# Waiting gathers and pairwise sums ahead of the transposes in a four-layer graph attention kernel

## Chip, cores and metric

The kernel runs on one core of a Trainium2 chip. The metric is the device time of one execution in microseconds (us), lower is better. Before the change it is 2476.21 us, the median of 11 runs (2470.24 to 2486.74).

## What is computed

A graph of 3327 nodes has features `x` (3327 x 256, float32) and a sparse adjacency matrix `adj` (3327 x 3327, int32, about 0.5% ones). Four layers run one after the other. Layer 0 is a graph attention with one score per neighbour. Layers 1 to 3 are transformer layers whose attention is masked by the graph. Cut to what matters:

```python
# layer 0
h = x @ Wt.T + bt
s = leaky_relu(h @ Wa.T + ba, 0.2)
w = softmax(where(adj > 0, s, -9e15), axis=1)
x = layernorm(x + (w @ h) @ Wp.T + bp)
# layers 1, 2, 3 (8 heads of 32)
q, k, v = split(layer_norm(x) @ w_qkv)
scores = where(adj != 0, q @ k.T * 32 ** -0.5, -inf)   # per head
out = softmax(scores) @ v                               # per head
x = x + out @ w_proj + b_proj
x = x + gelu(layer_norm(x) @ w1 + b1) @ w2 + b2
```

Row i of `out` is a sum over the neighbours of node i alone: each neighbour's 256 values, weighted per head.

## The kernel before

**Layer 0 and the lists.** The first part reads `adj` whole, computes layer 0, and makes for every node a list of its neighbours. The nodes are sorted by the number of neighbours and cut into 26 blocks of 128; `CAPS` has the longest list of each block, from 34 down to 9, 430 in all. Keys and values of layer 1 are written to a table in DRAM with one row of 512 floats (2 KB) per node, keys first.

**Attention by gathers.** Layers 1 to 3 work through the blocks in the order `ORDER`: lists of middle length first, rising to the longest, and the two blocks with the shortest lists last. For slot k of a block's lists, one indirect DMA that GpSimd issues (L640) fetches for each of the 128 nodes the table row of its k-th neighbour: 128 rows of 2 KB, a tile column of 128 x 512. A block's slots are cut into groups of 3 or 4 (`cuts`), 118 groups in a layer and 354 in all, and each group has a tile out of a pool of 12 (`SLOTS`). `Attend` has the steps of one block:

- `gather(g)` issues the group's 3 or 4 gathers.
- `scores(g)`: VectorE multiplies the keys by the query in place (L651) and sums over each head (L652).
- `exps` and `shares`: the softmax over the block's slots (L655 to L672). `shares` also opens the accumulator `po` in PSUM with a matrix product of zeros (L674).
- `values(oT, j)`: VectorE multiplies the group's values by their weights in place (L684). Then TensorE transposes each slot's two halves of 128 x 128 into the same `po`, adding up (L687). So the sum over neighbours is made by TensorE: two transposes a slot, 860 in a layer and 2580 in all. After the last group ScalarE copies `po` out (L693).

**The tail.** Blocks go on in pairs, the last two alone. `tail` is a generator that adds the projection, the norm, the feed-forward products (L567, L580) and, for layers 1 and 2, the keys and values of the next layer, which a scatter puts into the next table (L602). In layer 3 a scatter writes the output instead (L589). The norms raise to the power of -0.5 on GpSimd (L120). Pieces of tails are interleaved by `turn`.

**The order.** It is written out by hand in `layer` (`tc.manual_schedule`). Turn `now` handles one group: first the gathers of all groups up to `now + 3` (`AHEAD`) for which a slot tile is free are issued, then come `scores` of group `now`, a piece of each waiting tail, and `values` of the block before, spread over the turns. Each engine runs its instructions in this order. GpSimd's stream holds the gathers, in layer 1 the loads of node rows (L496), the powers, and the scatters. Each of its indirect DMAs signals its landing on one of eight semaphores in turn, and a gather waits for the one that used its semaphore before it, eight DMAs back.

Of the kernel before, what the change touches and what calls it, by code (L numbers as in the profile page):

```python
# [20 lines left out]
D = 256  # L21
# [25 lines left out]
SG = 4  # L47
SLOTS = 12
AHEAD = 3
NODES = 5  # L50
FH = FF // P // 2

# [5 lines left out]
def kernel(ctx: ExitStack, tc: tile.TileContext, ins, out: bass.AP):  # L58
    nc = tc.nc

    def wt(L, name):
        return ins[f"L{L}_gnn_{name}"]
# [47 lines left out]
    def moments(views, name):  # L110

        n = len(views)
        mv = small.tile([P, 4, 2], FP, tag="mv", name=f"mv_{name}")
        for j, v in enumerate(views):
            st = small.tile([P, 6], FP, tag="st", name=f"st_{name}_{j}")
            nc.vector.bn_stats(st, v)  # L116
            nc.vector.bn_aggr(mv[:, j, :], st)
        r = small.tile([P, 4], FP, tag="rsig", name=f"rsig_{name}")
        nc.vector.tensor_scalar(r[:, :n], mv[:, :n, 1], EPS, None, ALU.add)
        nc.gpsimd.tensor_tensor(r[:, :n], r[:, :n], mhalf[:, :n], ALU.pow)  # L120
        return mv, r

    def normed(pool, views, mv, rs, name):

        n = len(views)
        nm = small.tile([P, 4], FP, tag="nmu", name=f"nmu_{name}")
        nc.vector.scalar_tensor_tensor(nm[:, :n], mv[:, :n, 0], -1.0, rs[:, :n], ALU.mult, ALU.mult)  # L127
        xns = []
        for j, v in enumerate(views):
            xn = pool.tile([P, D], FP, tag="xn", name=f"xn_{name}_{j}")  # L130
            nc.scalar.activation(xn, v, AF.Identity, bias=nm[:, j:j + 1], scale=rs[:, j:j + 1])  # L131
            xns.append(xn)
        return xns
# [38 lines left out]
    with ExitStack() as st:  # L172
# [11 lines left out]
        for L in LAYERS:  # L184
            o = 16 * (L - 1)
            for k, name in ((0, "g1"), (2, "be1"), (4, "g2"), (6, "be2"), (8, "b1")):
                n = wt(L, name).shape[0] // P
# [71 lines left out]
        for g, blocks in enumerate(GROUPS):  # L259
            n = len(blocks)  # L260
# [210 lines left out]
    with ExitStack() as st:  # L471
# [12 lines left out]
        idx = keep.tile([P, NB, LW], U32, name="idx")  # L484
# [8 lines left out]
        def node_rows(b):  # L493

            nodes_[b] = work.tile([P, NODE], FP, tag="node", bufs=NODES, name=f"node_{b}")
            nc.gpsimd.indirect_dma_start(  # L496
                out=nodes_[b], out_offset=None, in_=node_dr[:, :],
                in_offset=bass.IndirectOffsetOnAxis(ap=perm[:, b:b + 1], axis=0))

        def node_list(b):  # L500

            t = nodes_[b]
            cd = t[:, 2 * D:2 * D + CAND]
            nr = (CAPS[b] + 7) // 8
            w = 8 * nr

            cg = work.tile([P, CAND], FP, tag="cg", name=f"cg_{b}")
            nc.vector.scalar_tensor_tensor(cg, cd, 0.0, segb.rearrange("p s k -> p (s k)"), ALU.is_gt, ALU.mult)
            nc.vector.tensor_add(cg, cg, cd)
            ls = work.tile([P, LW], FP, tag="ls", name=f"ls_{b}")  # L510
            for k in range(nr):
                nc.vector.max(out=ls[:, 8 * k:8 * k + 8], in_=cg)
                if k < nr - 1:
                    nc.vector.match_replace(out=cg, in_to_replace=ls[:, 8 * k:8 * k + 8], in_values=cg, imm_value=0.0)
            em = work.tile([P, LW], FP, tag="em", name=f"em_{b}")
            own = work.tile([P, 1], FP, tag="own", name=f"own_{b}")
            nc.vector.tensor_scalar(em[:, :w], ls[:, :w], 0.5, None, ALU.is_lt)
            nc.vector.tensor_scalar(own, pf[:, b:b + 1], 1.0, None, ALU.add)
            nc.vector.scalar_tensor_tensor(ls[:, :w], em[:, :w], own, ls[:, :w], ALU.mult, ALU.add)
            nc.vector.tensor_scalar(idx[:, b, :w], ls[:, :w], -1.0, None, ALU.add)  # L520
            nc.vector.tensor_scalar(bias[:, b, :w], em[:, :w], NEG, None, ALU.mult)
            nc.vector.tensor_reduce(found[:, b, 0:1], em[:, :w], AX.X, ALU.add)
            nc.scalar.copy(found[:, b, 1:2], t[:, 2 * D + CAND:])
            nc.scalar.copy(x_sb[:, b, :], t[:, :D])
# [8 lines left out]
        def tail(L, w, wqn, blocks, oT):  # L533
# [15 lines left out]
            mv, rs = moments(views, f"f{tag}")  # L549
            yield AHEAD  # L550
            xns = normed(work, views, mv, rs, f"f{tag}")
# [41 lines left out]
            mv, rs = moments(views, f"h{tag}")  # L593
            yield AHEAD
            xns = normed(work, views, mv, rs, f"h{tag}")
# [20 lines left out]
        class Attend:  # L616
# [19 lines left out]
            def gather(self, g):  # L636
                a, z = self.cuts[g]
                t = slots.tile([P, SG, 2 * D], FP, tag="slot", name=f"sl_{self.tag}_{g}")
                for k in range(a, z):
                    nc.gpsimd.indirect_dma_start(  # L640
                        out=t[:, k - a, :], out_offset=None, in_=kv_dr[self.L][:, :],
                        in_offset=bass.IndirectOffsetOnAxis(ap=idx[:, self.b, k:k + 1], axis=0))
                self.tiles.append(t)

            def scores(self, g):
# [31 lines left out]
            def values(self, oT, j):  # L677

                g = self.vdone
                a, z = self.cuts[g]  # L680
                n = z - a
                t = self.tiles[g]
                vv = t[:, :n, D:].rearrange("p s (h d) -> p s h d", h=HEADS)
                nc.vector.tensor_mul(vv, vv, self.pw[:, a:z, :, None].to_broadcast([P, n, HEADS, HD]))  # L684
                for k in range(n):
                    for c in range(2):
                        nc.tensor.matmul(self.po[:, c, :], t[:, k, D + c * P:D + (c + 1) * P], ident,  # L687
                                         is_transpose=True, start=False,
                                         stop=(a + k == self.S - 1 and c == 1))
                self.vdone += 1  # L690
                if self.vdone < len(self.cuts):
                    return False
                nc.scalar.copy(oT[:, :, j * P:(j + 1) * P], self.po)  # L693
                return True

        place = {b: (m, j) for m, blocks in enumerate(CHUNKS) for j, b in enumerate(blocks)}
        tails = []
        hidden = []

# [9 lines left out]
        def layer(L):  # L709
# [10 lines left out]
            if first:  # L720
                for b in ORDER[:NODES - 2]:
                    node_rows(b)
# [17 lines left out]
            for k, a in enumerate(att):  # L740
# [3 lines left out]
                for g in range(n):  # L744
                    if first and g == 0:
                        if k + NODES - 2 < NB:
                            node_rows(ORDER[k + NODES - 2])
                        for m in ((1, 2) if k == 0 else (k + 2,)):
                            if m < NB:
                                node_list(ORDER[m])  # L750
                    while sent < turns and held < SLOTS and sent - now <= AHEAD:
                        todo[sent][0].gather(todo[sent][1])
# [219 lines left out]
```

## Time and profile before

| | |
|---|---|
| median of 11 runs | 2476.21 us |
| the profiled execution | 2476.94 us |
| its span, first to last instruction | 2475.1 us |
| VectorE (DVE) busy | 1781.7 us, 72% |
| TensorE (PE) matrix products busy | 1663.3 us, 67% |
| GpSimd (POOL) busy | 1442.7 us, 58% |
| ScalarE (ACT) busy | 769.1 us, 31% |
| gathers (L640) | 1290, 3.7 us median from issue to landing |
| software DMA queue | 363.51 MB, 50.0% of the 16 engines' span |

The profile shows one execution, with times in us from the start of the span. Busy time is the time in which an engine ran an instruction of the program; a DMA that GpSimd issues is busy on GpSimd while it makes the DMA's descriptors, and the transfer itself runs on the 16 DMA engines. `out<-in` names the tile written and the tiles read; `sl` is a group's tile, `kv` a table of keys and values, `po` the sum over neighbours. A bracket at the end of a timeline row has the idle time of the engine ahead of the instruction, and what ended it; "issue" there means that the engine waited for nothing that the profile shows. A time from issue to landing runs from the start of the instruction on GpSimd to the semaphore that tells that all the data are there.

### The profile page before, as it was taken

What the parts mean: (1) busy time and instruction counts of PE and PEld (TensorE: products, weight loads), DVE (VectorE), ACT (ScalarE), POOL (GpSimd) and SP (SyncE); (2) the same over time, 40 slices, a digit from 0 to 9 for tenths busy, and PEclk for the clock granted to TensorE, in tenths of its full rate; (3) what the DMA queues carried; (4) which work ended last, traced back from release to release, by engine and by line L of the source; (5) the groups of instructions that cost most, each with busy time, mean ns of one, the idle gap of its engine ahead of it and who ended that gap; (6) DMA issues with size and microseconds to landing.
All of it is one profiled execution on the core that took longest, in us unless ns stands there. A gap on an engine that the chain in (4) does not pass through costs nothing. (4 is left out here: it accounts for less than half of the span.)

```text
span 2475.1 us, 25607 instructions
## 1 busy us (share of the span) xinstructions
PE 1663.3 (67%) x8349; PEld 1303.3 (53%) x8349; DVE 1781.7 (72%) x3203; ACT 769.1 (31%) x1420; POOL 1442.7 (58%) x1632
## 2 busy tenths in 40 slices
PE   5687851666786667682787787767826767766566
PEld 5556530555565555561565565555625655544455
DVE  3898956877778888726867878787357777777772
ACT  2787820223332222240332422232302322211222
POOL 0111116766667777517766777776167777777761
PEclk9899975687888887795788888778957878877778
DMA  6466416756567777507766677776076666666660
GB/s 236 152 231 214 149 66 194 209 169 191 178 193 206 209 212 209 157 32 255 202 194 195 187 218 214 209 212 183 26 221 201 202 192 200 199 202 184 198 182 11
DMA packets 154568, 451.22 MB, mean 182 GB/s; under 512 B 30576, under 2 KB 57850, under 8 KB 151098
## 3 DMA queue, kind: packets, MB, share of 16 engines
q0 software_dynamic: 111168, 363.51, 50.0%
q1 hardware_dynamic: 38462, 80.03, 9.4%
q10 hardware_dynamic: 4794, 5.94, 0.7%
q8 instruction: 69, 1.13, 0.2%
q14 instruction: 75, 0.61, 0.1%
HBM read 410.48 MB, written 38.88 MB: 182 GB/s over the span
## 5 line engine op out<-in xcount | busy, mean ns | idle before, releaser
L640 POOL DMA_INDIRECT sl<-kv,idx x1290 | 1230.7, 954 | 405.6 <-issue 322.9
L687 PE MATMUL po<-ident,sl 128*128 128x128 f32 x2580 | 475.7, 348 | 603.2 <-DVE sl L684 602.5
L687 PEld LDWEIGHTS po<-ident,sl 128*128 128x128 f32 x2580 | 397.6, 181 | 672.4 <-DVE sl L684 623.3
L651 DVE TENSOR_TENSOR sl<-sl,qp 128x1024 f32<-128x1024 f32 (+1 forms) x354 | 397.0, 1121 | 229.5 <-DMA sl<-kv,idx 172.0
L652 DVE TENSOR_REDUCE sc<-sl 128x32 f32<-128x1024 f32 (+1 forms) x354 | 398.2, 1125 | 12.0
L684 DVE TENSOR_TENSOR sl<-sl,qp 128x1024 f32<-128x1024 f32 (+1 forms) x354 | 389.0, 1119 | 2.6
L567 PE MATMUL pu<-fT,w 128*128 128x256 f32 (+1 forms) x1344 | 326.0, 391 | 38.0 <-ACT fT L143 38.0
L580 PE MATMUL pd<-w,gT 128*128 128x256 f32 x1248 | 324.0, 416 | 24.4 <-ACT gT L571 24.4
L580 PEld LDWEIGHTS pd<-w,gT 128*128 128x128 f32 x1248 | 256.2, 211 | 75.4 <-ACT gT L571 28.3
L567 PEld LDWEIGHTS pu<-fT,w 128*128 128x128 f32 x1344 | 253.9, 205 | 78.3 <-ACT fT L143 46.8
L571 ACT ACTIVATE gT<-pu,pv 128x256 f32<-128x256 f32 (+1 forms) x336 | 135.0, 456 | 267.3 <-PE pu L567 266.5
L161 PE MATMUL pk<-wq,hT 128*128 128x512 f32 x312 | 167.7, 664 | 3.1 <-ACT hT L143 3.1
L131 ACT ACTIVATE xn_f<-x_sb,nmu_f,rsig_f 128x256 f32<-128x256 f32 x78 | 42.8, 593 | 361.3 <-DVE nmu_f L127 347.3
L585 DVE TENSOR_TENSOR x_sb<-x_sb,pd 128x512 f32<-128x512 f32 (+1 forms) x42 | 27.2, 648 | 164.4 <-PE pd L580 164.4
L693 ACT COPY oT<-po 128x256 f32<-128x256 f32 x78 | 29.0, 372 | 373.4 <-PE po L687 373.1
L548 DVE TENSOR_TENSOR x_sb<-x_sb,pp 128x512 f32<-128x512 f32 (+1 forms) x42 | 27.2, 648 | 129.1 <-PE pp L546 129.0
L423 DVE MAX8 cand<-abf 128x8 f32<-128x256 bf16 x338 | 119.1, 410 | 0.0
L401 POOL MEMSET abf<- 128x1 bf16 x26 | 2.5, 100 | 192.9 <-DVE cand L423 165.2
L602 POOL DMA_INDIRECT kv<-kvr,perm x52 | 52.3, 1005 | 90.2 <-ACT kvr L163 78.3
L413 ACT ACTIVATE aT<-pt 128x1024 bf16<-128x1024 bf16 x104 | 85.0, 874 | 13.9 <-PE pt L412 13.9
L161 PEld LDWEIGHTS pk<-wq,hT 128*128 128x128 f32 x312 | 61.9, 215 | 51.5 <-issue 36.9
L166 PE MATMUL pq<-wq,hT 128*128 128x256 f32 x312 | 83.6, 392 | 7.2 <-ACT kvr L163 7.2
(217 smaller groups left out, 1959.4 us busy)
## 6 DMA issues: line engine op xcount, KB each, us to landing
a<-in_adj_dram SPq DMA_DIRECT2D x25, 1663.5 KB
sl<-kv,idx POOLq DMA_INDIRECT x1290, 3.7
kv<-kvr SPq DMA_DIRECT2D x26, 256.0 KB
q<-qr SPq DMA_DIRECT2D x52, 128.0 KB
q<-q SPq DMA_DIRECT2D x52, 128.0 KB
w<-in_L_gnn_w_dram SPq DMA_DIRECT2D x6, 1024.0 KB
node<-x SPq DMA_DIRECT2D x26, 128.0 KB
node<-qr SPq DMA_DIRECT2D x26, 128.0 KB
```

The costliest lines, as they stand in the source:

```text
L161: nc.tensor.matmul(pk, hT[:, c, :], wq[:, c, D:], start=(c == 0), stop=(c == 1))
L166: nc.tensor.matmul(pq[:, :D], hT[:, c, :], wq[:, c, :D], start=(c == 0), stop=(c == 1))
L413: nc.scalar.activation(aT[:, k0:k0 + kn, :], pt[:, :kn, :], AF.Sign)
L423: nc.vector.max(out=cand[:, 8 * m:8 * m + 8], in_=ab3[:, m, :])
L567: nc.tensor.matmul(pu[:, a, :n * P], w["w1"][:, c, f * P:(f + 1) * P], fT[:, c, :n * P], start=(c == 0), stop=(c == 1))
L571: nc.scalar.activation(gT[:, f0 + a, :n * P], pu[:, a, :n * P], AF.Gelu_apprx_tanh, bias=pv[:, L - 1, 8 + f:9 + f])
L580: nc.tensor.matmul(pd[:, j, :], gT[:, f, j * P:(j + 1) * P], w["w2"][:, h * FH + f, :], start=False, stop=(h == 1 and f == FH - 1 and j == ...
L640: nc.gpsimd.indirect_dma_start(out=t[:, k - a, :], out_offset=None, in_=kv_dr[self.L][:, :], in_offset=bass.IndirectOffsetOnAxis(ap=idx[:, ...
L651: nc.vector.tensor_mul(kq, kq, self.qp[:, None, :D].to_broadcast([P, n, D]))
L652: nc.vector.tensor_reduce(self.sc[:, a:z, :], kq.rearrange("p s (h d) -> p s h d", h=HEADS), AX.X, ALU.add)
L684: nc.vector.tensor_mul(vv, vv, self.pw[:, a:z, :, None].to_broadcast([P, n, HEADS, HD]))
L687: nc.tensor.matmul(self.po[:, c, :], t[:, k, D + c * P:D + (c + 1) * P], ident, is_transpose=True, start=False, stop=(a + k == self.S - 1 ...
```

## The change

It has two parts. First, a list `flight` holds the gathers issued last. From the third gather on, each one waits for the landing of the gather two before it. The list runs on over groups, blocks and layers; node loads and scatters are not in it. Second, after the values of a group are weighted, VectorE adds the last n // 2 slots of the group's n to its first n // 2 in place. For a group of four, two slots are left; for a group of three, the third is added to the first, and two are left. Only these are transposed into `po`.

```diff
+FLIGHT = 2
...
                 for k in range(a, z):
-                    nc.gpsimd.indirect_dma_start(
+                    ins = nc.gpsimd.indirect_dma_start(
                         out=t[:, k - a, :], out_offset=None, in_=kv_dr[self.L][:, :],
-                        in_offset=bass.IndirectOffsetOnAxis(ap=idx[:, self.b, k:k + 1], axis=0))
+                        in_offset=bass.IndirectOffsetOnAxis(ap=idx[:, self.b, k:k + 1], axis=0)).ins
+                    if len(flight) == FLIGHT:
+                        tc.add_manual_dep(ins, flight.pop(0).name,
+                                          mybir.DependencyInfo(mybir.DependencyClass.Sync, mybir.DependencyReason.DATA),
+                                          reason="gathers in flight")
+                    flight.append(ins)
                 self.tiles.append(t)
...
                 nc.vector.tensor_mul(vv, vv, self.pw[:, a:z, :, None].to_broadcast([P, n, HEADS, HD]))
-                for k in range(n):
+                m = n // 2
+                nc.vector.tensor_add(t[:, :m, D:], t[:, :m, D:], t[:, n - m:n, D:])
+                for k in range(n - m):
                     for c in range(2):
                         nc.tensor.matmul(self.po[:, c, :], t[:, k, D + c * P:D + (c + 1) * P], ident,
                                          is_transpose=True, start=False,
-                                         stop=(a + k == self.S - 1 and c == 1))
+                                         stop=(z == self.S and k == n - m - 1 and c == 1))
...
+        flight = []
         tails = []
```

## The prediction

> **What bounds the kernel now.** I read the groups of instructions first, then the gather line by itself, then GpSimd's timeline, and last the busy time by layer. The groups (busy us, mean ns of one, idle time before and its releaser):
>
> ```profile
> L640 POOL DMA_INDIRECT sl<-kv,idx x1290 | 1230.7, 954 | 405.6 <-issue 322.9
> L687 PE MATMUL po<-ident,sl 128*128 128x128 f32 x2580 | 475.7, 348 | 603.2 <-DVE sl L684 602.5
> L684 DVE TENSOR_TENSOR sl<-sl,qp 128x1024 f32<-128x1024 f32 (+1 forms) x354 | 389.0, 1119 | 2.6
> ```
>
> The gathers hold GpSimd for 1230.7 us, and most of its idle time ahead of them, 322.9 us, has no cause that the profile shows. The timeline of GpSimd in layer 1 tells what that is:
>
> ```profile
> 1003.48 0.95 POOL L640 DMA_INDIRECT sl<-kv,idx  x1 [0.30 <-issue]
> 1004.73 0.95 POOL L640 DMA_INDIRECT sl<-kv,idx  x1 [0.30 <-issue]
> 1005.98 0.94 POOL L640 DMA_INDIRECT sl<-kv,idx  x1 [0.30 <-issue]
> ```
>
> A gather is 0.95 us of work and 0.30 us of gap, so one starts every 1.25 us, with no wait for any landing. A gather is in the air for longer than that; the gather line by itself says how long:
>
> ```profile
> L640 POOL DMA_INDIRECT sl<-kv,idx x1290: 942/949/1194, 391.7 to 2407.6; - x185
> DMA to landing us min/median/max: 3.3/3.7/6.5
> ```
>
> 3.7 us counts from the start of the issue. VectorE's first product of layer 1 confirms it: it starts 3.78 us after the start of its group's last gather.
>
> ```profile
> 394.19 1.01 POOL L640 DMA_INDIRECT sl<-kv,idx  x1 [0.30 <-issue]
> ...
> 397.97 0.95 DVE L651 TENSOR_TENSOR sl<-sl,qp 128x768 f32<-128x768 f32 x1 [1.74 <-DMA sl<-kv,idx]
> ```
>
> So about three gathers fly at once (3.7 / 1.25). The streams, first gather to last, are seen in these rows (and 391.7 and 2407.6 above):
>
> ```profile
> 1040.53 0.95 POOL L640 DMA_INDIRECT sl<-kv,idx  x1 [0.30 <-issue]
> ...
> 1119.92 0.99 POOL L640 DMA_INDIRECT sl<-kv,idx  x1 [2.94 <-issue]
> ...
> 1727.95 0.95 POOL L640 DMA_INDIRECT sl<-kv,idx  x1 [0.30 <-issue]
> ...
> 1808.08 0.98 POOL L640 DMA_INDIRECT sl<-kv,idx  x1 [2.54 <-issue]
> ```
>
> They last 648.8, 608.0 and 599.6 us, against 430 x 1.25 = 538 us of pure issue; the rest is node loads, scatters and short stalls. After each stream comes a drain without gathers: 79.4, 80.1 and 67.5 us. With the 391.7 us ahead, that makes the span: 391.7 + 1856.4 + 227.0 = 2475.1.
>
> **Part 1, the wait.** It removes nothing. It adds to each gather a wait for the landing of the second one before. How fast GpSimd starts after a landing is shown by the output scatters of layer 3, of which each second one already waits for the first to land:
>
> ```profile
> 2448.23 1.05 POOL L589 DMA_INDIRECT out_dram<-x_sb,perm  x1 [10.13 <-DVE x_sb L585]
> 2450.95 0.99 POOL L589 DMA_INDIRECT out_dram<-x_sb,perm  x1 [1.67 <-DMA out_dram<-x_sb,perm]
> ```
>
> In the trace the first lands at 2450.68, so the restart takes 0.27 us; of the eleven pairs whose wait was ended by the landing, nine show 0.27 and two 0.80. I take 0.27.
>
> A gather then starts at best one landing plus 0.27 us after the second before it, so two gathers take landing + 0.27 us. What is the landing with only one other in the air? Sorting the 1290 by how many indirect DMAs were still flying at their start: 58 had one (median 3.48 us), 957 had two (3.66), 236 had three (3.67). Fewer in flight helps little. The two-in-flight rows have a mean 0.07 above their median; waits add up means, so I take 3.48 + 0.07 = 3.55 us. The pace is (3.55 + 0.27) / 2 = 1.91 us a gather instead of 1.25, and 430 gathers take 821.3 us a layer.
>
> The Trainium skill, "DMA: Bandwidth & Descriptors", section "Anatomy of one DMA — SWDGE (gpsimd) path", gives a fit for this path of about 2.0 us plus the bytes at 436 GB/s. For 256 KB an estimate by it is 2.6 us, a pace of (2.6 + 0.27) / 2 = 1.44 us, and the whole sum below would come to some 2540 us. The trace's 3.3 at the least speaks against it, and I go by the trace.
>
> What is queued behind the waiting gather on GpSimd: node loads, powers and scatters. Two gathers use 2 x 1.25 of their 3.82 us, so 1.32 us is free for them. A power (0.7 us) fits and is hidden by the wait. A node load or key scatter (1.25 to 1.3 us) fits in one of the two gaps if that one is wide, and pushes one chain by up to 1.3 us if it is not; I take 0.6. Between first and last gather there are 42 of these in layer 1 (25 us) and 20 in layer 2 (12 us). In layer 3 there are 11 pairs of output scatters; one holds GpSimd for 2.72 + 0.99 + 0.30 = 4.0 us, of which 1.3 is free: 11 x 2.7 = 30 us. Extras: 67 us. Streams after: 3 x 821.3 + 67 = 2531 us, against 1856.4: **+674.5 us**. This takes stalls of the old stream on other engines as gone: with 3.64 gathers in a group, a turn lasts 7.0 us, and what GpSimd waits for was begun a turn earlier.
>
> **Part 2, the adds.** The groups are 228 of four and 126 of three. Removed: 4 transposes in a group of four and 2 in a group of three, 912 + 252 = 1164 of 2580, or 45% of the 475.7 us: 215 us less on TensorE. Added: one VectorE add per group, 128x512 or 128x256. The nearest rows are the adds to `x_sb` (L548, 128x512 0.69 us, 128x256 0.42 us): 228 x 0.69 + 126 x 0.42 = 210 us more on VectorE. Both lie beside the gathers. In the three layers (391 to 2475 us) VectorE is busy 1497.4 us: with the adds (1497.4 + 210) / 354 = 4.8 us a turn, TensorE (1406.0 - 215) / 354 = 3.4 us, against 7.0 us of gathering. So both edits cost and bring nothing in the streams. The cover is the wait itself; without it VectorE would have 1707 us of work in 2084.
>
> **The drains.** Now VectorE multiplies the last group's keys (1052.39) 11.9 us after that group's last gather starts (1040.53), of which 3.7 is the landing: at the end of a layer it is behind by 8 us, because the longest block's nine groups of values are weighted beside the last two blocks' short lists. Slower gathers would let it catch up (8 us less in each layer), the nine adds put back 9 x 0.69 = 6 us, and the six of the last two blocks some 3. I take 0, with ends of -24 and +27 us in all.
>
> **Sum.** 2475.1 + 674.5 = 3149.6 us of span. The profiled execution took 1.8 us more than its span and 0.7 us more than the median: 3149.6 + 1.8 - 0.7 = **3150 us** (3150.7, rounded).
>
> **Rivals.**
> - *Gathers land much sooner when fewer fly.* For it: each landing time holds some queueing. Against: the least of 1290 is 3.25 us, and 14 that started with none in flight have a median of 3.42. With 3.25 for all: 1290 x 0.15 = 194 us less, 2957.
> - *The restart is slow.* If the 0.80 us of two of the eleven rows held for all: 1290 x 0.265 = 342 us more, 3490. It would need a reason that nine rows of eleven do not have.
> - *Not slower: the wait never ends last.* This would be so where the gather two back is home by the time GpSimd is free again, 2.5 us after that one's start: landing + 0.27 below 2.5, so a landing under 2.23 us; or where the wait were for the issue and not the landing. Then the adds decide: 2.3% of the span (57 us) is transposes in the chain that ended last, 45% of it 26 us; and 1.5% (37 us of 389) is the weighting, so one tenth of the adds' 210 us comes back as 21. That gives 2471. Against it: no gather of 1290 is under 3.25, and in the program's order the third gather waits for the semaphore that the first one's landing signals.
>
> **How the numbers follow.** My forecast 85%, sooner landings 6%, slow restart 6%, no binding wait 3%. Within the forecast the landing lies between 3.42 (the median with none in flight: -84 us) and 3.73 (the mean with two: +116 us); with the drains' ends, 3150 - 84 - 24 = 3042 and 3150 + 116 + 27 = 3293. So the range is 3040 to 3290, and leaves out the three rivals and a little of my own case. A difference of 0.2%, about 5 us, is what a measurement of this kernel can tell from none. Faster 0.01, the same 0.01 (both from the last rival), slower 0.98.
>
> **What would show it.** The gather row's idle time should grow from 405.6 to about 1200 us with the gather's own landing named as releaser; gathers should start in steps whose pairs add up to 3.8 us; landing median 3.5; VectorE's idle time should be ended by landing gathers far more than the 172.0 us of now; transposes 1416; DMA share in the streams down from 0.62 by a third, since the bytes stay. The forecast is wrong if the pairs are much under 3.6 or over 4.1 us, if drains move by more than 10 us each, or if GpSimd still stalls on other engines in the streams.

## The result, and the profile after

| | before | after |
|---|---|---|
| median | 2477.14 us (31 runs) | 3201.19 us (8 runs, 3197.31 to 3209.05) |
| ratio, 95% interval | | 1.2922 (1.2903 to 1.294) |
| span of the profiled execution | 2475.1 us | 3198.3 us |
| the three streams of gathers | 648.8, 608.0, 599.6 us | 859.9, 843.7, 869.9 us |
| the three drains | 79.4, 80.1, 67.5 us | 87.3, 85.0, 62.7 us |
| granted TensorE clock, mean | 0.80 | 0.71 |

The changed kernel is 29% slower. Nearly all of it lies in the streams, 717 us of 724. The page's groups, as for the kernel before (busy us, mean ns of one, idle time before and its releaser):

```profile
L641 POOL DMA_INDIRECT sl<-kv,idx x1290 | 1248.7, 968 | 1168.3 <-DMA sl<-kv,idx 875.5
L695 PE MATMUL po<-ident,sl 128*128 128x128 f32 x1416 | 350.2, 394 | 1178.2 <-DVE sl L692 1178.2
L692 DVE TENSOR_TENSOR sl<-sl 128x512 f32<-128x512 f32 (+1 forms) x354 | 211.6, 598 | 12.2
```

The gathers' work is nearly what it was (1230.7 us before; the 18 us more are explained at run 2), but the idle time ahead of them has nearly tripled, from 405.6 us, and now a gather's landing ends most of it. The transposes are 1416, and the adds take 211.6 us. Landings, from the gather line by itself:

```profile
L641 POOL DMA_INDIRECT sl<-kv,idx x1290: 942/952/1502, 389.8 to 3135.6; - x185
DMA to landing us min/median/max: 3.1/3.4/7.2
```

and GpSimd's timeline in layer 1:

```profile
1021.59 1.02 POOL L641 DMA_INDIRECT sl<-kv,idx  x1 [1.36 <-DMA sl<-kv,idx]
1023.56 0.95 POOL L641 DMA_INDIRECT sl<-kv,idx  x1 [0.95 <-DMA sl<-kv,idx]
1025.22 0.95 POOL L641 DMA_INDIRECT sl<-kv,idx  x1 [0.72 <-DMA sl<-kv,idx]
1027.08 0.95 POOL L641 DMA_INDIRECT sl<-kv,idx  x1 [0.91 <-DMA sl<-kv,idx]
1028.84 0.94 POOL L641 DMA_INDIRECT sl<-kv,idx  x1 [0.81 <-DMA sl<-kv,idx]
```

Read every second row: 1021.59, 1025.22, 1028.84 are 3.63 and 3.62 us apart. That is a landing and a restart. The gap of 0.30 us that the rows showed before is 0.7 to 1.4 us in these, and has a releaser. VectorE feels the same from the other end; in the list of waits it stands for gathers 792.5 us instead of 172.0 (the first two lines are of the kernel before):

```profile
POOL sl L640 <- DMA sl<-kv,idx: 40.2, 132, 0.3
DVE sl L651 <- DMA sl<-kv,idx: 172.0, 103, 5.5
...
POOL sl L641 <- DMA sl<-kv,idx: 875.5, 852, 5.1
DVE sl L657 <- DMA sl<-kv,idx: 792.5, 254, 21.1
```

And the busy time of layer 2 (busy us and count of each engine, clock, DMA share, GB/s) has a DMA share of 0.48 where it was 0.63 (before, then after):

```profile
1137.00:1800.00 663.00, 482.73 (x2186) 377.60 (x2187) 481.65 (x696) 193.37 (x384) 442.11 (x470) 0.81 0.63 185
...
1380.00:2285.00 905.00, 506.80 (x1798) 359.12 (x1798) 546.57 (x801) 195.22 (x386) 450.92 (x472) 0.71 0.48 139
```

So no engine and no DMA queue is busy all the time: what bounds is a latency, waited for with two in flight. Runs 3, 4 and 8 test this.

### The profile page after: what moved, and what is told of

Its sections match the earlier page's. It is cut to its first block, busy times and chain, and to the rows that moved or that the text cites. A ratio compares the mean times of both kernels' runs of the same rounds, so it can differ in the third digit from the quotient of the medians.

```text
span 3198.3 us, 23628 instructions
## 1 busy us (share of the span) xinstructions
PE 1713.1 (54%) x7185; PEld 1243.5 (39%) x7185; DVE 2002.9 (63%) x3557; ACT 768.5 (24%) x1420; POOL 1463.5 (46%) x1632
## 5 line engine op out<-in xcount | busy, mean ns | idle before, releaser
L641 POOL DMA_INDIRECT sl<-kv,idx x1290 | 1248.7, 968 | 1168.3 <-DMA sl<-kv,idx 875.5
L695 PE MATMUL po<-ident,sl 128*128 128x128 f32 x1416 | 350.2, 394 | 1178.2 <-DVE sl L692 1178.2
L657 DVE TENSOR_TENSOR sl<-sl,qp 128x1024 f32<-128x1024 f32 (+1 forms) x354 | 398.0, 1124 | 804.4 <-DMA sl<-kv,idx 792.5
L695 PEld LDWEIGHTS po<-ident,sl 128*128 128x128 f32 x1416 | 227.6, 196 | 1297.0 <-DVE sl L692 1245.9
L568 PE MATMUL pu<-fT,w 128*128 128x256 f32 (+1 forms) x1344 | 383.9, 442 | 75.7 <-ACT fT L144 75.7
L581 PE MATMUL pd<-w,gT 128*128 128x256 f32 x1248 | 385.1, 474 | 61.9 <-ACT gT L572 61.9
L581 PEld LDWEIGHTS pd<-w,gT 128*128 128x128 f32 x1248 | 300.5, 248 | 133.3 <-ACT gT L572 66.2
L568 PEld LDWEIGHTS pu<-fT,w 128*128 128x128 f32 x1344 | 295.5, 237 | 131.2 <-ACT fT L144 83.9
L692 DVE TENSOR_TENSOR sl<-sl 128x512 f32<-128x512 f32 (+1 forms) x354 | 211.6, 598 | 12.2
L162 PE MATMUL pk<-wq,hT 128*128 128x512 f32 x312 | 187.7, 733 | 10.5 <-ACT hT L144 10.5
L547 PE MATMUL pp<-w_proj,oT 128*128 128x256 f32 x312 | 107.3, 501 | 0.3
L668 ACT ACTIVATE sc<-sc 128x136 f32<-128x136 f32 (+11 forms) x78 | 24.4, 313 | 301.6 <-DVE sc L667 297.4
```

The source lines that it names most:

```text
L162: nc.tensor.matmul(pk, hT[:, c, :], wq[:, c, D:], start=(c == 0), stop=(c == 1))
L547: nc.tensor.matmul(pp[:, j, :], oT[:, c, j * P:(j + 1) * P], w["w_proj"][:, c, :], start=False, stop=(c == 1 and j == n - 1))
L568: nc.tensor.matmul(pu[:, a, :n * P], w["w1"][:, c, f * P:(f + 1) * P], fT[:, c, :n * P], start=(c == 0), stop=(c == 1))
L581: nc.tensor.matmul(pd[:, j, :], gT[:, f, j * P:(j + 1) * P], w["w2"][:, h * FH + f, :], start=False, stop=(h == 1 and f == FH - 1 and j == ...
L641: ins = nc.gpsimd.indirect_dma_start(out=t[:, k - a, :], out_offset=None, in_=kv_dr[self.L][:, :], in_offset=bass.IndirectOffsetOnAxis(ap= ...
L657: nc.vector.tensor_mul(kq, kq, self.qp[:, None, :D].to_broadcast([P, n, D]))
```

## Experiments

The theory, **A**: the pace of the streams is landing plus restart over the number in flight, and the adds lie beside it. Rivals: **B**, the adds are much of the cost; **C**, waiting itself has a fixed price, landed or not. Each comparison's median of the kernel before was 2479 (runs 1 to 4), 2486 (5 to 8) and 2476 us (10 to 12) on three chips; run 9 stands apart.

### 1. The wait without the adds

```diff
-                m = n // 2
-                nc.vector.tensor_add(t[:, :m, D:], t[:, :m, D:], t[:, n - m:n, D:])
-                for k in range(n - m):
+                for k in range(n):
```

> The wait of part 1 without the adds of part 2: all 2580 transposes are back. Theory A (landings set the pace): a gather's pace is half of landing plus restart, and neither TensorE's 215 us nor VectorE's 210 us are on that path, so 3150 to 3250 us, within 2% of the changed kernel's 3201, with the gathers' streams of some 855 us a layer. Rival B (the adds cost much of it, by VectorE's 210 us or by the sum waiting between product and transposes): 210 us less than the changed kernel or lower, below 3000 us.

Measured: 3179.84 us, ratio 1.2828 (1.2806 to 1.285). Streams 858.1, 849.0 and 871.0 us, drains 76.2, 73.3 and 57.8. The wait alone makes 701 of the 724 us; B falls. Though TensorE has 1164 transposes more, it is 0.7% faster than the changed kernel, and all of that is in the drains: 207 us in the sum, against 235 with the adds and 227 before.

### 2. The adds without the wait

The diff is part 2 of the change alone.

> The adds of part 2 without the wait. Theory A: gathers start every 1.25 us as before, streams of 600 to 650 us; the transposes saved on the path (26 us of the 57 us that are in the chain) and the adds that come onto it (21 us) nearly cancel: 2450 to 2500 us, my value 2471. Rival B (the adds cost): 2476 + 210 = 2690 us if VectorE's added time came onto the path in full.

Measured: 2577.48 us, ratio 1.0391 (1.0374 to 1.0409). This is a miss, and lies between both theories: the adds cost 97 us where nothing hides them. Streams grew by 69 us and drains by 30. VectorE's wait for gathers fell to 73.8 us; instead, GpSimd waits longer for VectorE's norms before it can raise to a power:

```profile
POOL rsig_f L120 <- DVE rsig_f L119: 110.0, 25, 13.5
POOL rsig_h L120 <- DVE rsig_h L119: 80.6, 18, 11.4
```

These were 72.4 and 70.0 us before. Gathers stand behind those powers in GpSimd's stream. But that is less than half of what the streams lose: inside them GpSimd's waits ahead of powers grew by 25 us and those ahead of key scatters by 6, while the gathers' own work grew by 34 us (1227.8 to 1261.7). 98 gathers took 1.05 us or more, up to 1.48; in the kernel before 7 did, up to 1.19. 92 of the 98 ran beside an add of VectorE that had begun before them:

```profile
637.57 0.69 DVE L686 TENSOR_TENSOR sl<-sl 128x512 f32<-128x512 f32 x1
637.68 1.41 POOL L640 DMA_INDIRECT sl<-kv,idx  x1 [0.30 <-issue]
```

The longer the add still has to run, the longer the gather takes: 1.10 us in the mean with 0.2 to 0.3 us of the add left, 1.26 with 0.4 to 0.5 and 1.44 with 0.6 to 0.7, so it ends about 0.83 us after the add. The 14 that begin with the add, 0.7 us or more of it left, take 0.95. Gathers that begin beside VectorE's products (L651, L684) take 0.95 to 0.96 us as always. The adds read two inputs of a group's tile in SBUF, while the second input of these products lies in PSUM; no run shows that this is the reason.

### 3. and 4. Four and one in flight

```diff
-FLIGHT = 2
+FLIGHT = 4     # run 3
+FLIGHT = 1     # run 4
```

> The changed kernel with four gathers in flight in place of two. Theory A: a gather lands 3.7 us after its start, and restart included 3.95 us lie below 4 x 1.25 = 5.0 us, so the wait never ends last: 2450 to 2500 us, as with the adds alone. Rival C (it is the waiting itself that costs, a fixed price for each gather that waits on a second semaphore, landed or not): the changed kernel's 724 us over 1290 gathers is 0.56 us each, and stays: about 3200 us.

> The changed kernel with one gather in flight. Theory A: the pace is landing plus restart itself. With none in flight 3.35 to 3.45 us of landing; restart 0.26 us for gathers with one wait (904 of 1290) and 0.75 us for those with two or more (386), 0.41 us in the mean: 1290 x 3.8 = 4900 us, plus 390 ahead, 235 of drains and some 20 for the output scatters' pairs: 5400 to 5600 us. Rival C: about 3200 us, since each gather waits as often as before. A third, that the DMA engines' work is the limit and not the latency: the same bytes in the same time, about 3200 us.

Measured: with four 2582.65 us (ratio 1.0413, 1.0395 to 1.0432), the same as the adds alone (2577.48 us); with one 5465.46 us (one execution). Run 3 misses its 2450 to 2500 us as run 2 did, by the cost of the adds. C falls with it: the waits are all still there and hardly ever end last (a landing ends 142 of the gathers' idle times, and 132 in the kernel before). C and the third theory, the DMA engines' work, also fall with run 4. Idle time ahead of the gathers with four:

```profile
  issue: 326.1, 1044
  DMA sl<-kv,idx: 50.3, 142
```

With one, GpSimd's timeline shows landing and restart alone, 3.57, 3.60 and 4.10 us from start to start:

```profile
1002.95 0.95 POOL L641 DMA_INDIRECT sl<-kv,idx  x1 [3.07 <-DMA sl<-kv,idx]
1006.52 0.95 POOL L641 DMA_INDIRECT sl<-kv,idx  x1 [2.62 <-DMA sl<-kv,idx]
1010.12 0.95 POOL L641 DMA_INDIRECT sl<-kv,idx  x1 [2.65 <-DMA sl<-kv,idx]
1014.22 0.95 POOL L641 DMA_INDIRECT sl<-kv,idx  x1 [3.15 <-DMA sl<-kv,idx]
```

Landings have a mean of 3.36 us there. Of the 1260 starts that a landing released, 926 came 0.26 us after it and 334 came 0.75 us after: 0.39 in the mean, and 3.36 + 0.39 = 3.75 us. The streams (4874.3 us) give 3.78 us a gather.

### 5. and 6. What the adds cost and the transposes bring, apart

Run 5 keeps all transposes and writes the sums where nobody reads them. Run 6 has 1416 of the 2580 transposes and no adds, so it leaves the last n // 2 slots of each group's values out of the output.

```diff
 # run 5, on the kernel before
+                m = n // 2
+                nc.vector.tensor_add(t[:, :m, :D], t[:, :m, D:], t[:, n - m:n, D:])
                 for k in range(n):
 # run 6, on the adds alone
-                nc.vector.tensor_add(t[:, :m, D:], t[:, :m, D:], t[:, n - m:n, D:])
```

> The kernel before with VectorE's 354 adds in their place and of their size, but written over the group's keys, which nobody reads any more: all 2580 transposes stay and none waits for an add. Theory D1 (VectorE's time in its queue costs): the 97 us of the adds alone or somewhat more, since TensorE keeps its 215 us: 2570 to 2630 us. Rival D2 (what costs is TensorE: fewer transposes leave it idle and its granted clock falls from 0.80 to 0.76, or the transposes wait for the adds): the cost goes, 2476 to 2510 us.

> The kernel before with 1416 of its 2580 transposes and no adds: the last half of each group's weighted values is left out of the sum. Theory D1: the transposes alone are worth something between nothing and the 26 us of my working: 2450 to 2476 us. Rival D2 (a less busy TensorE gets a lower clock, and its products in the tails take longer): 2490 to 2550 us, with a granted clock near 0.76.

Measured: run 5 2565.99 us, ratio 1.0322 (1.0299 to 1.0345); run 6 2467.18 us, ratio 0.992 (0.9903 to 0.9938). The groups of run 5, with no transpose waiting for an add:

```profile
L686 DVE TENSOR_TENSOR sl<-sl 128x512 f32<-128x512 f32 (+1 forms) x354 | 212.3, 600 | 12.1
L689 PE MATMUL po<-ident,sl 128*128 128x128 f32 x2580 | 494.0, 354 | 659.2 <-DVE sl L684 657.6
```

VectorE's 212 us alone cost 80 us, with the granted clock at 0.794. That is 4 us under D1's range and far above D2's, so most of the cost is the adds' time on VectorE. It isn't only their time in VectorE's queue: of the 61 us by which the streams grew, 32 are again the gathers' own work, longer beside adds. The 1164 transposes alone are worth 19 us, within the 0 to 26 of the working, though the clock fell to 0.774. Alone the two make +61 us; together they make +97. The other 36 us need both (transposes that wait for the adds, or the lower clock of 0.76); the runs do not part these.

### 7. The wait for a free tile, taken by another instruction

```diff
-                t = slots.tile([P, SG, 2 * D], FP, tag="slot", name=f"sl_{self.tag}_{g}")
+                whole = slots.tile([P, SG * 2 * D + 2], FP, tag="slot", name=f"sl_{self.tag}_{g}")
+                nc.gpsimd.memset(whole[:, SG * 2 * D:SG * 2 * D + 1], 0.0)
+                t = whole[:, :SG * 2 * D].rearrange("p (s d) -> p s d", s=SG)
```

This asks about the restart. In the changed kernel 379 gathers wait for two or more semaphores, and the sequencer of GpSimd has 386 extra instructions for them; 679 of the starts that a landing released came 0.26 us after it, and 280, of which 272 are of those gathers, came 0.75 us after. The gather line of the changed kernel:

```profile
L641 POOLq EVENT_SEMAPHORE  x386: 17/17/3902, 396.9 to 3131.8; - x193
```

> The changed kernel, with a one-column memset by GpSimd ahead of each group's gathers, in a spare column of the group's tile. The memset takes the waits for the tile to come free, so gathers with two or more waits fall from 379 to 63. Theory E (a gather that waits for a landing and something else starts 0.75 us after the landing and not 0.26): 280 such starts less, each 0.49 us, on one of two chains: 70 us less than 3201, and some 10 to 20 us back for 354 memsets of 0.1 us: 3130 to 3160 us. Rival (the tile really comes free so late): 3190 to 3220 us.

Measured: 3141.35 us, ratio 1.2636 (1.2607 to 1.2665), 60 us less than the changed kernel (70 by the ratios, as the two ran on different chips). The gather line of run 7:

```profile
L643 POOLq EVENT_SEMAPHORE  x63: 17/17/17, 401.8 to 3070.3; - x63
```

Restarts of 0.75 us fell from 280 to 21 (1019 at 0.26). So the second wait has a price of its own, and only on a gather that has to wait for the landing. In the changed kernel's trace the price hangs on where the landing's wait stands. In 303 gathers the extra instruction carries it: 279 of them start 0.74 to 0.80 us after the landing, and none sooner. In 32 the gather itself carries it and the extra instruction another wait: 24 of these start 0.26 us after.

### 8. Gathers of half the bytes

```diff
-                        out=t[:, k - a, :], out_offset=None, in_=kv_dr[self.L][:, :],
+                        out=t[:, k - a, :D], out_offset=None, in_=kv_dr[self.L].rearrange("n (h d) -> (n h) d", h=2),
...
-                vv = t[:, :n, D:].rearrange("p s (h d) -> p s h d", h=HEADS)
+                vv = t[:, :n, :D].rearrange("p s (h d) -> p s h d", h=HEADS)
```

> The changed kernel with gathers of half the bytes: rows of 1 KB, 128 KB a gather; the keys' half of another row is read, and the values' work is done on it, so the values proper are left out. Everything else is as in the changed kernel. Theory A (latency): the 16 DMA engines spend 39.3% of 3198 us on 1394 software DMAs, 0.9 us for each, so half the bytes can take at most 0.45 us off the landing's 3.43: landing 3.0 to 3.4 us, time 2910 to 3190 us. Rival (bytes set the landing): landing halves to 1.7 us, the pace falls back to 1.25 us, time 2470 to 2580 us. The Trainium skill's fit in DMA: Bandwidth & Descriptors, section Anatomy of one DMA, gives a slope of 0.3 us for 128 KB, an estimate of 3.13 us of landing and 3007 us.

Measured: 2885.7 us (one execution), and landings of

```profile
DMA to landing us min/median/max: 2.6/2.8/6.7
```

The landing is mostly fixed: half the bytes take 0.61 us off the mean (3.43 to 2.82). That is more than the 0.45 expected from the DMA engines' busy time, so the time fell below the expected 2910; but it is far from half. The fit of the Trainium skill (DMA: Bandwidth & Descriptors, Anatomy of one DMA) has a slope of 0.30 us for these 128 KB, half of what is measured; what the two means leave as the fixed part is an estimate of 2.82 - 0.61 = 2.21 us, close to its 2.0. The times here run from the start of the issue, of which 0.95 us is GpSimd's own work.

### 9. Three in flight, on a chip that was different

```diff
-FLIGHT = 2
+FLIGHT = 3
```

> The changed kernel with three gathers in flight. Theory A: the pace is landing plus restart over three, (3.7 + 0.26) / 3 = 1.32 us, 0.07 above the issue's 1.25, and 0.16 more where the restart is 0.75. With the adds GpSimd already waits for VectorE in part (streams of 1925 us against 1290 x 1.25 = 1613), so part of the 1290 x 0.07 = 90 us is hidden: 2580 to 2670 us, that is 0 to 90 us above the adds alone (2577). Rival (a wait for a landing costs by itself, however many fly): nearer to 3200 than to 2577.

Measured: 2815.23 us. But in this comparison the kernel before took 3100.93 us in the median of seven runs (3087.94 to 3106.97) on a chip that no other run came to, so three in flight with the adds were faster there: ratio 0.9091 (0.9038 to 0.9144). By the theory this run was to take 2580 to 2670 us.

### 10. to 12. Three in flight again, with and without the adds, and the kernel before

Run 10 has run 9's edit and run 1's, run 11 is run 9 again, and run 12 is the kernel before.

> Three gathers in flight, without the adds. In the last comparison the kernel before itself took 3101 us and not 2480, on another chip, and three in flight with the adds 2815. Theory A on a chip like the first two (the kernel before near 2480): pace 1.32 us in place of 1.25, 2480 to 2570 us. Theory G (on the other chip gathers land late when many fly, and the limit helps): where the kernel before takes near 3100, this one takes 2700 to 2815 us, faster than with the adds.

> Three gathers in flight with the adds, the same kernel as in the last comparison. On a chip where the kernel before takes near 2480: 2580 to 2670 us, 0 to 90 us above the adds alone, by theory A. Where the kernel before takes near 3100: about 2815 us again.

> The kernel before, unchanged, for its profile on the same chip as the two others. Where it takes near 2480: the rows shown, a landing of 3.7 us in the median and streams of 649, 608 and 600 us. Where it takes near 3100: theory G expects longer landings or more DMA time a packet, and streams some 200 us longer a layer; the rival, a slower chip altogether, expects layer 0 and the drains to be longer too.

Measured, on a chip where the kernel before took 2476.28 us: run 10 2625.83 us, ratio 1.0616 (1.0592 to 1.0639); run 11 2688.14 us, 1.0869 (1.0844 to 1.0895); run 12 2478.7 us. Both of the first two miss their expectation, by 56 and 18 us: three in flight cost 150 us without the adds and 111 on top of them. Run 10's streams are 2003.7 us, 147 more than before. A landing of 3.68 us (the mean here) and a restart of 0.26 are only 0.2 us over 3 x 1.25 = 3.75, but with a restart of 0.75 they are 0.7 over. In run 10's trace 243 late restarts held GpSimd 134 us longer than the issue's gap of 0.30 us, 0.55 us each, and 155 early ones 37 us. The expectation had divided the extra 0.49 us of a late restart by the three gathers in flight, which leaves 0.16; by the trace a late one costs 0.3 us more than an early one.

The different chip of run 9 was not met again. Run 11 is the same kernel, so their traces can be compared: layer 0 (392.5 us on run 9's chip, 393.3 here), the drains (251.2 and 252.4) and the third stream (676.8 and 675.9) are the same; only the first two streams are longer, 760.4 and 728.2 us against 696.4 and 665.2. So that chip was not slower throughout, and the rival of run 12's expectation doesn't fit. Late landings (theory G) are not shown either: run 9's trace has no landings, and its DMA packets took as long in the first two streams (177 and 161 ns in the mean) as in run 11 (176 and 157). Why the kernel before took 3100 us there, and what holds up these two streams, is **open**: there is no profile of the kernel before from that chip.

## Why the prediction was right

The mechanism, the sign and the size were right: 3201 us is 51 us over the 3150 forecast and inside 3040 to 3290. By its steps:

- **The pace.** Forecast 1.91 us a gather from a landing of 3.55 and a restart of 0.27. Measured: the landing's mean is 3.43, the restart's 0.40 (679 of 0.26 and 280 of 0.75): 1.92. Two errors of the sum cancel: 1290 x 0.12 / 2 = 77 us less, and the long restarts, which run 7 prices at 60 us, more. That they nearly cancel is luck. The prediction saw two restarts of 0.80 in eleven and put them in a rival with the words "It would need a reason that nine rows of eleven do not have". The reason stands in the program's order: three gathers in ten wait for a second semaphore, and most of these have the landing's wait on the extra instruction.
- **The extras.** Streams of 2531 us were forecast, 3 x 821.3 + 67, and 2573.5 were measured. The trace splits them start by start, by the time from the landing that a gather waits for to its start, halved because two chains run side by side. Landings and restarts of 0.26 make 2383 us, and the late restarts add 74. Starts behind an output scatter add 40 us (30 in the forecast), and those behind node loads, key scatters and powers about 50 (37). Another 28 us are gathers that follow the one before at the pace of the issue, because that one was late; the forecast had no term for these.
- **The fewer in flight, the sooner the landing.** 3.75 with up to three (kernel before), 3.43 with two, 3.36 with one: right that it helps little.
- **The adds and the transposes beside the gathers.** Right: with the wait, both together cost 21 us (3201 against 3180), and not in the streams. The working named the wait as the cover; run 2 takes the cover away, and they cost 97 us. Its 210 us for the adds came out as 211.6. Its 215 us less on TensorE came out as 125.5 (475.7 to 350.2), as a transpose took 394 ns instead of 348 at the lower clock.
- **The drains.** 0 was taken, with ends of -24 and +27. Run 1 shows the first end (-20, VectorE catches up) and the difference to it the second (+28, the adds at the end of a layer, where VectorE is late). Their sum is +8.
- **The signs.** Most came as said: idle time ahead of the gathers 1168.3 us, landing median 3.4, drains moved by less than 10 us each. The DMA share fell by less than a third (0.63 to 0.48). And one sign of being wrong did show: VectorE and TensorE end 175 us of the gathers' idle time, where it was 41 before. Little of it is a term of its own, since the landing's wait covers it: only 19 of these 142 starts came more than 0.8 us after the landing, and they make 11 us of the streams. But 106 of the 142 are late restarts, which run 7 takes away.
- **The last rival's price was wrong.** For a wait that never ends last it gave 2471 us, from shares of the chain of waits: a tenth of VectorE's added time coming back. Run 3 is that rival built, and takes 2583 us. The step that failed there is "one tenth of the adds' 210 us comes back as 21": run 5 shows 80 of 212. The share of the chain counts only the steps that ended last in the kernel before. Time added to VectorE, busy for 72% of it, also moves the steps that it releases (the powers on GpSimd and the gathers behind them), lengthens the drains by 24 us, and makes gathers that begin beside an add longer, a term that the working did not have (32 us in run 5).

## What to carry to other kernels

A limit on transfers in flight sets a pace of landing plus restart over the limit. Compare that with the pace of the issue before setting it: here (3.4 + 0.4) / 2 = 1.9 us against 1.25 us, and only from four on was the limit free. Work moved from an engine with slack to the busiest one costs even when the other engine is relieved of as much; the chain of waits underprices it, and the busier engine can also slow another's instructions, as the adds did the gathers. And an instruction that waits for a late event should wait for nothing else: a cheap instruction ahead of it can take the other waits.

## What the runs showed of the hardware

- GpSimd starts an indirect DMA 0.26 us after the landing it waits for, and 0.74 us or more after if an extra semaphore instruction ahead of the DMA carries that wait (303 gathers of the changed kernel).
- A gather that begins while VectorE runs an add of two inputs in SBUF works longer, until about 0.83 us after the add's end: up to 1.48 us instead of 0.95 (run 2). Beside products with one input in PSUM it doesn't.
- An indirect gather of 128 rows lands 3.36 us after its start in the mean when alone and 3.43 with one other in flight if the rows have 2 KB, and 2.82 us after, with one other in flight, if they have 1 KB.
- The less of the time TensorE was busy, the lower was its granted clock: 0.80 before (67% busy), 0.75 with the wait alone (56%), 0.71 in the changed kernel (54%) and 0.63 with one in flight (34%). One product of the feed-forward part (`pu`) took 391 ns in the mean before and 442 ns after. In the streams this cost nothing that shows: 2573 us in the changed kernel, at 0.71, and 2578 with the wait alone, at 0.75.
- One chip ran the kernel before 25% slower than the others in all of seven runs; see run 9.
